# A state-space scan between an FFN and an attention on one Trainium2 core: fixed order on four engines, a quarter of the scaling as products with diagonals, and the last batch's softplus summed by TensorE

## The chip, the cores and the metric

The kernel runs on one core of one Trainium2 chip. The metric is the device time of one execution in microseconds (us). The engines are TensorE (PE, with its weight loads as PEld), VectorE (DVE), ScalarE (ACT), GpSimd (POOL) and SyncE (SP, which here only issues DMAs).

## The reference, cut to what matters

Four sublayers follow each other, each with a layer norm in front and a residual around it: a causal attention, a gated FFN with ternary weights, a selective state-space scan, and a second attention with a mixture of experts. All is float32. The change concerns the scan and what prepares it. B = 4 batches of T = 512 tokens with C = 512 channels, 16 states per channel:

```python
xz = einsum('btd,rd->btr', u, W_xproj)          # u = layernorm(x); 128 + 16 + 16 columns
delta = softplus(einsum('btr,dr->btd', xz[..., :128], W_dt) + b_dt)
dA = exp(delta[..., None] * -exp(A_log))        # [b, t, d, n]
Bu = delta[..., None] * B_mat[:, :, None, :] * u[..., None]
h_t = dA_t * h_(t-1) + Bu_t                     # along the 512 tokens
y_t = sum_n h_t * C_t[:, None, :]
x = x + y + u * D_param
```

## The kernel before, in words

The residual stream stays in SBUF as `xs[b]`, tokens on partitions: four tiles of 128 tokens by 512 channels per batch. The scan works on channels by tokens, since the scan instruction runs along the free dimension.

**FFN (L593 to L706).** One batch after another, eleven slices `f` of the hidden width. `gated` (L643) puts 16 matmuls into a pair of PSUM banks (the PSUM holds two such pairs and four single banks), then SiLU, product and casts follow on ACT and DVE; `down` (L663) multiplies by w2 one slice later. Between the slices, a generator `prepare` (L494) for the batch before is advanced by a number of steps that the list in L690 gives, and from slice 4 on also `inputs` (L610) for the next batch. Only PE's order is the program's; on the other engines a scheduler places the instructions.

**`prepare(b)`** normalizes the batch into `row_s` and adds u * D to x on POOL (L507, L508), transposes to `uT`, multiplies by W_xproj (`pd` of 128 rows, `pb` of 32 rows, L528), transposes the B columns to tokens (`pbt`, L539) into `bts`, and stores the C rows to DRAM (`c_rows`). Softplus is computed as max(z, 0) + ln(1 + e) with e = exp(-|z|), with the rounding of 1 + e put right: `e` from Abs and Exp on ACT (L551, L554), max(z, 0) in `delta` (L552), u = (e + 1) - 1 (L558), e - u (L559), added (L560), ln (L562), added (L567). delta goes to DRAM (`deltas`), delta * uT (`ux`, L570) is transposed and goes to DRAM as `dxs`. For the last batch `prepare` runs during the scan (L887), one step for every second scan step (L912).

**Scan (L805 to L954).** The eight PSUM banks are single: four for the sums of a batch, four for the rest. There are 128 steps (b, n, half): 4 batches, 16 states, and two halves of the channels. For each (b, n), `scale` (L823) runs eight instructions on ACT: four scalings of the token tiles of `dxT` by the B column (`bu`, L829) and four exponentials for dA (`da`, L835; two buffers). For each step, `turn` (L838) transposes 2 x 4 blocks into two banks; `scan` (L848) runs two scan instructions on DVE; `weigh` (L856) multiplies both by the C row (`cb`, a broadcast load from `c_rows`, L859) on POOL into `hc`; `add_up` (L867), two steps behind, transposes eight blocks on PE and sums them over n in the four banks, which are added to x at a batch's end (L882). `h` and `hc` have three buffers. `fetch` (L816) loads `delta_l` and `dxT` of a batch, 1 MB each; the first is asked for after the FFN (L884), the others at n = 3 of the batch before.

The order within the scan: PE's is written out (L889); DVE, ACT and POOL are placed by the scheduler, and SP's queue of DMAs too. From step 56 on the preparation's room is given to the next attention's weights (L918 to L949, 14 DMAs), and from step 78 on `enter` (L715) of the second attention's batch 0 is advanced at every third step: statistics, rows, squares, and transposes of its input.

Of the kernel before, what the change touches and what calls it, by code (L numbers as in the profile page):

```python
# [15 lines left out]
ALU = mybir.AluOpType  # L16
# [29 lines left out]
def block_kernel(ctx: ExitStack, tc: tile.TileContext, a: dict, out: bass.AP):  # L46
# [45 lines left out]
    deltas = tc.dram_tile([B, C, T], F32, name="deltas")  # L92
    dxs = tc.dram_tile([B * T, C], F32, name="dxs")


# [385 lines left out]
    dpar = sw.tile([P, C], F32, tag="dpar", name="dpar")  # L481

    def scan_constants(pool):

        nc.scalar.activation(am, am, AF.Exp)
        nc.vector.tensor_scalar(am, am, -1.0, None, ALU.mult)
        dp = half_pair("dp")
        for k in range(NK):
            diag = pool.tile([P, P], F32, tag="diag", name="diag")
            nc.vector.tensor_scalar(diag, ident, dcol[:, k : k + 1], None, ALU.mult)  # L490
            nc.tensor.matmul(dp[:, k * P : (k + 1) * P], ones, diag, start=True, stop=True)
        nc.scalar.copy(dpar, dp)

    def prepare(b, pool, spot, ahead):  # L494
# [29 lines left out]
        yield  # L524

        pb = spot("pb")
        for k in range(NK):
            nc.tensor.matmul(  # L528
                pb[: 2 * NS, :], wx[:, k, RANK:], uT[:, k, :], start=k == 0, stop=k == NK - 1
            )  # L530
            if k == 1:
                yield
        bcT = pool.tile([2 * NS, T], F32, tag="bcT", name="bcT")
        nc.scalar.copy(bcT, pb[: 2 * NS, :])
        nc.sync.dma_start(c_rows[b], bcT[NS:, :])
        yield
        pb = spot("pbt")
        for t in range(NT):
            nc.tensor.transpose(  # L539
                pb[:, t * NS : (t + 1) * NS], bcT[:NS, t * P : (t + 1) * P], ident[:NS, :NS]  # L540
            )
        nc.scalar.copy(bts[:, b, :], pb[:, : NT * NS])
        yield
# [43 lines left out]
        yield  # L587

    def half_pair(name):
        return pair(name)[:, 0, :]  # L590


    with tc.tile_pool(name="b_s", bufs=1) as bs, tc.tile_pool(name="b_1", bufs=1) as b1, tc.tile_pool(  # L593
# [16 lines left out]
        def inputs(b, mv=None):  # L610

            high = b2.tile([P, NK, T], F32R, tag="hTh", name="hTh")
            low = b2.tile([P, NK, T], F32R, tag="hTl", name="hTl")
            high_low[b] = high, low
# [56 lines left out]
        with tc.manual_schedule(engines={mybir.EngineType.PE}):  # L671
# [4 lines left out]
            for b in range(B):  # L676
# [7 lines left out]
                for f, rows in enumerate(FROWS):  # L684
                    pending.append((f, rows, gated(b, f, rows, hT)))
                    if b == 0 and f + 3 < NF:
                        quantize_down(f + 3)
                    if b == 0 and f == 6:
                        clear()
                    for _ in range((2, 3, 2, 2, 2, 3, 3, 3, 3, 4, 3)[f]):  # L690
                        next(between, None)
                    if f >= 4:
                        next(coming, None)
                    if b == 0 and f == 4:
                        scan_constants(b2)
                    if len(pending) > lag:
                        if ys is None:
                            ys = [bank(f"y{t}") for t in range(NT)]
                        down(b, *pending.pop(0), ys)
# [14 lines left out]

    def enter(b, pool):  # L715

# [16 lines left out]
        hT = far.tile([P, NK, T], F32, tag="hT", name="hTd")  # L733
        before = None
        for t in range(NT + 1):
            row = None
            if t < NT:
                row = pool.tile([P, C], F32, tag="row", name="row_d", bufs=2)
                nc.vector.scalar_tensor_tensor(
                    row, hs[b][:, t, :], rs[:, t : t + 1], ln1, ALU.mult, ALU.mult  # L740
                )
            if before is not None:
                transpose_into(hT, before, (t - 1) * P)
            before = row
            yield
# [59 lines left out]
    eight("s")  # L805
    with tc.tile_pool(name="c_f", bufs=2, reuse_waits="tile") as cf, tc.tile_pool(
        name="c_1", bufs=1
    ) as c1, tc.tile_pool(name="c_2", bufs=2) as c2:

        das = [c1.tile([P, NK, T], F32, tag=f"da{i}", name=f"da{i}") for i in range(2)]  # L810
        for da in das:
            nc.vector.memset(da[:, :, 0:1], 0.0)
        steps = [(b, n, half) for b in range(B) for n in range(NS) for half in range(2)]
        loaded, scaled, decays, turned, states, weighed, sums = {}, {}, {}, {}, {}, {}, {}

        def fetch(b):  # L816
            delta = cf.tile([P, NK, T], F32, tag="delta_l", name="delta_l")
            nc.sync.dma_start(delta, by_rows(deltas[b]))
            dxT = cf.tile([P, NT, C], F32, tag="dxT", name="dxT")
            nc.sync.dma_start(dxT, by_tokens(dxs, b))  # L820
            loaded[b] = delta, dxT

        def scale(b, n):  # L823

            delta, dxT = loaded[b]
            rows = []
            for t in range(NT):
                row = c2.tile([P, C], F32, tag=f"bu{t}", name=f"bu{t}")
# [8 lines left out]

        def turn(b, n, half):  # L838
            bu = [bank("bu") for _ in range(2)]
            for i in range(2):  # L840
                k = 2 * half + i
                for t in range(NT):
                    nc.tensor.transpose(  # L843
                        bu[i][:, t * P : (t + 1) * P], scaled[b, n][t][:, k * P : (k + 1) * P], ident
                    )
            turned[b, n, half] = bu

# [19 lines left out]
        def add_up(b, n, half):  # L867
# [3 lines left out]
            for i in range(2):  # L871
                k = 2 * half + i
                for t in range(NT):
# [5 lines left out]
                    )  # L879
            if n == NS - 1 and half == 1:  # L880
                for t in range(NT):
                    nc.vector.tensor_tensor(xs[b][:, t, :], xs[b][:, t, :], sums[b][t], ALU.add)  # L882

        fetch(0)  # L884
        last = ExitStack()
        cp = last.enter_context(tc.tile_pool(name="c_p", bufs=1, side="right", reuse_waits="tile"))
        between = prepare(B - 1, cp, bank, 4)  # L887
        come = enter(0, c1)
        with tc.manual_schedule(engines={mybir.EngineType.PE}):  # L889
            for _ in range(2):  # L890
                next(between)
            scale(0, 0)
            for _ in range(5):
                next(between)
            turn(*steps[0])
            for m, (b, n, half) in enumerate(steps):
                if half == 0:
                    if n + 1 < NS:
# [5 lines left out]
                if m + 1 < len(steps):  # L904
                    turn(*steps[m + 1])
                scan(b, n, half)
                weigh(b, n, half)
                if m >= 2:
                    add_up(*steps[m - 2])

                if m % 2 == 1:
                    next(between, None)  # L912
                if m == 56:
                    for _ in between:
# [34 lines left out]
                    ln1 = held("ln1", [P, C], a["ln1_w"].partition_broadcast(P))  # L949

                if m >= 76 and m % 3 == 0 and m < 76 + 3 * 13:
                    next(come)
            for step in steps[-2:]:
                add_up(*step)  # L954


# [538 lines left out]
```

## Time and profile before

| | us |
|---|---|
| Four runs: median (lowest, highest) | 1977.81 (1973.01, 1981.5) |
| Profiled execution: own time | 1977.9 |
| Profiled execution: span of the profile | 1976.2 |
| FFN's last matmul ends | 757.55 |
| First scan instruction starts | 768.98 |
| Step 58 starts (its first scan, the 117th) | 943.5 |
| Last scan instruction ends | 1120.1 |

All points in time are counted from the start of the span. A row of a table of busy times gives a stretch, its length, and the busy time of each engine with its instructions in brackets. A row of a timeline gives the start, the time until the last of the merged instructions ends, the engine, the line, the operation with output and inputs, and their number; in square brackets the idle time before it and who ended it. Instructions of one engine overlap a little, so prices are taken from start to start. In PE's rows a float32 matmul stands as two records and a transpose as one. Lines are of the kernel before unless the changed kernel is named.

### The profile page before, as it was taken

To read this page: it belongs to the slowest core of one execution; us is meant where nothing else is said; L and a number is where in the kernel's file an instruction comes from. 1 tells how busy PE (TensorE), PEld (TensorE's weight loads), DVE (VectorE), ACT (ScalarE), POOL (GpSimd) and SP (SyncE) were. 2 spreads that over 40 slices of the span, in tenths; PEclk is the share of its full clock that TensorE was granted. 3 is DMA by queue.
4 is the path that set the end of the run, shared out by engine and by line. 5 is a ranking of instruction groups with operands and counts; after the bars stand their busy time and mean duration, and the time that the engine had idled before them with its cause. 6 is when DMAs were issued, how large, how long until landed. Compare 5 with 4: busy or idle time off the path is not lost. (4 is left out here: it accounts for less than half of the span.)

```text
span 1976.2 us, 26953 instructions
## 1 busy us (share of the span) xinstructions
PE 1798.0 (91%) x10030; PEld 1084.9 (55%) x10030; DVE 1151.9 (58%) x1909; ACT 946.6 (48%) x1941; POOL 581.1 (29%) x390
## 2 busy tenths in 40 slices
PE   7999999989999897867887889999999999999997
PEld 3443343347666665656776655555565554545453
DVE  6456445675463737999999856664636543422223
ACT  3434433332243436978999646655646442111110
POOL 3221212110202205868998710001000000144431
PEclk9999999999999999989999979999979889999999
DMA  7003200110010104134311100010100106244446
GB/s 242 8 1 105 61 1 1 44 45 31 1 43 1 43 1 157 47 107 121 109 55 49 28 1 1 7 38 1 44 11 28 38 22 202 80 92 90 92 74 191
DMA packets 70885, 114.25 MB, mean 58 GB/s; under 512 B 7962, under 2 KB 26778, under 8 KB 70756
## 3 DMA queue, kind: packets, MB, share of 16 engines
q1 hardware_dynamic: 59796, 88.02, 13.7%
q0 software_dynamic: 8656, 20.32, 5.5%
q10 hardware_dynamic: 2304, 4.20, 0.6%
q8 instruction: 81, 1.33, 0.3%
q14 instruction: 48, 0.39, 0.1%
HBM read 81.18 MB, written 31.33 MB: 57 GB/s over the span
## 5 line engine op out<-in xcount | busy, mean ns | idle before, releaser
L862 POOL TENSOR_TENSOR hc<-h,cb 128x1024 f32<-128x1024 f32 x128 | 303.4, 2422 | 42.4 <-DVE h L851 26.3
L851 DVE TENSOR_TENSOR_SCAN h<-da,bu 128x512 f32<-128x512 f32 x256 | 290.0, 1197 | 14.4 <-ACT da L835 8.2
L843 PE MATMUL bu<-ident,bu 128*128 128x128 f32 x1024 | 163.8, 286 | 59.4 <-DVE h L851 36.0
L270 PE MATMUL pq<-wqkv,hT 128*128 128x512 f32 x384 | 181.8, 622 | 1.1 <-ACT hT L131 1.1
L843 PEld LDWEIGHTS bu<-ident,bu 128*128 128x128 f32 x1024 | 119.2, 144 | 94.3 <-ACT bu L829 55.1
L835 ACT ACTIVATE da<-delta_l,am 128x511 f32<-128x511 f32 x256 | 164.9, 723 | 3.6 <-DVE h L851 3.6
L829 ACT ACTIVATE bu<-dxT,bts 128x512 f32<-128x512 f32 x256 | 164.8, 723 | 0.5 <-PE bu L843 0.5
L875 PE MATMUL ys<-ident,hc 128*128 128x128 f32 x1024 | 140.8, 281 | 12.2 <-POOL hc L862 9.1
L1080 ACT ACTIVATE pr<-scd,nm 128x128 f32<-128x128 f32 (+3 forms) x256 | 133.0, 527 | 35.1 <-DVE nm L1077 31.1
L648 PE MATMUL pg<-hTh,w 128*128 128x512 f32 (+1 forms) x352 | 139.7, 397 | 2.9 <-DVE sil L654 2.1
L648 PE MATMUL pg<-hTl,w 128*128 128x512 f32 (+1 forms) x352 | 139.1, 395 | 0.2 <-DVE hTl L638 0.2
L1382 PE MATMUL pgr<-wgu,gTe 128*128 x304 | 137.1, 593 | 0.0
L875 PEld LDWEIGHTS ys<-ident,hc 128*128 128x128 f32 x1024 | 118.6, 145 | 20.9 <-POOL hc L862 16.1
L1069 PE MATMUL scd<-qkTd 32*128 32x512 f32 (+3 forms) x512 | 117.3, 541 | 12.2 <-ACT pr L1080 9.3
L270 PEld LDWEIGHTS pq<-wqkv,hT 128*128 128x128 f32 x384 | 72.3, 197 | 95.8 <-issue 87.1
L350 ACT ACTIVATE pt<-sc 128x1024 f32<-128x1024 f32 (+3 forms) x128 | 84.1, 698 | 83.8 <-PE sc L345 81.3
L1092 PEld LDWEIGHTS tpd<-ident,pr 128*128 128x128 f32 x640 | 74.7, 152 | 68.7 <-issue 35.8
L1092 PE MATMUL tpd<-ident,pr 128*128 128x128 f32 x640 | 109.0, 305 | 2.1 <-DVE ptd L1097 1.5
L101 POOL TENSOR_TENSOR ri_ln<-ri_ln,minus_half 128x4 f32<-128x4 f32 (+1 forms) x17 | 16.9, 994 | 308.0 <-DVE ri_ln L100 303.9
L1077 DVE TENSOR_REDUCE nm<-scd 128x2 f32<-128x256 f32 (+3 forms) x128 | 104.2, 814 | 0.0
L1072 DVE TENSOR_TENSOR scd<-scd,neg 128x256 f32<-128x256 f32 x128 | 54.9, 430 | 81.9 <-PE scd L1069 79.3
L351 POOL TENSOR_SCALAR_AFFINE_SELECT pt<-pt 128x512 f32<-128x512 f32 x64 | 43.4, 679 | 194.7 <-ACT pt L350 194.7
(258 smaller groups left out, 3164.6 us busy)
## 6 DMA issues: line engine op xcount, KB each, us to landing
cb<-c_rows SPq DMA_DIRECT2D x64, 256.0 KB, 3.2
q_w<-in_w2T SPq DMA_DIRECT2D x20, 256.0 KB, 2.9
deltas<-delta SPq DMA_DIRECT2D x16, 256.0 KB, 2.1
dxs<-st SPq DMA_DIRECT2D x16, 256.0 KB, 2.5
delta_l<-deltas SPq DMA_DIRECT2D x4, 1024.0 KB, 9.8
dxT<-dxs SPq DMA_DIRECT2D x4, 1024.0 KB, 6.9
acc<-h SPq DMA_DIRECT2D x16, 256.0 KB, 2.0
hrows<-h SPq DMA_DIRECT2D x4, 1024.0 KB, 4.3
```

Source lines behind the costliest of these rows:

```text
L270: nc.tensor.matmul(y, inputs_T[b][:, k, t * P : (t + 1) * P], wqkv[:, k, s * C : (s + 1) * C], start=k == 0, stop=k == NK - 1,)
L648: nc.tensor.matmul(pg[:rows, i, :], w[:, k, f * P : f * P + rows], part[:, k, :], start=k + m == 0, stop=k + m == NK,)
L829: nc.scalar.activation(row, dxT[:, t, :], AF.Copy, scale=bts[:, b, t * NS + n : t * NS + n + 1])
L835: nc.scalar.activation(da[:, k, 1:], delta[:, k, 1:], AF.Exp, scale=am[:, k, n : n + 1])
L843: nc.tensor.transpose(bu[i][:, t * P : (t + 1) * P], scaled[b, n][t][:, k * P : (k + 1) * P], ident)
L851: nc.vector.tensor_tensor_scan(h[:, i, :], decays[b, n][:, 2 * half + i, :], bu, 0.0, ALU.mult, ALU.add)
L862: nc.gpsimd.tensor_tensor(hc, states.pop((b, n, half)), weighed[b, n].unsqueeze(1).to_broadcast([P, 2, T]), ALU.mult)
L875: nc.tensor.matmul(sums[b][t][:, k * P : (k + 1) * P], hc[:, i, t * P : (t + 1) * P], ident, is_transpose=True, start=n == 0 and k == 0, s ...
L1069: nc.tensor.matmul(sc[:, i, :w], qkT[at, g, t * P : w], qkT[at, NG + g, :w], start=True, stop=True)
L1080: nc.scalar.activation(pr[:, i, :w], sc[:, i, :w], AF.Exp, bias=nm[:, i : i + 1], accum_out=sums[b, g][:, t, 2 * p + i : 2 * p + i + 1],)
L1092: nc.tensor.transpose(tp[:, j * P : (j + 1) * P], pr[:, i, j * P : (j + 1) * P], ident)
L1382: nc.tensor.matmul(pg, gT[:, k, :], wgu[:, bass.ds(e, 1), k, :].rearrange("p e o -> p (e o)"), start=k == 0, stop=k == NK - 1,)
```

## The change

- During the scan, the order of PE, DVE, ACT and POOL is that of the program. SP's queue is still placed by the scheduler.
- Token tile 0 is no longer scaled on ACT. `keep_inputs` makes, for each n, the 128x128 diagonal of the B column of tile 0 (one DVE instruction of 128x2048 per batch), stores all to DRAM (`diags`, 1 MB per batch), and `scale` loads one (64 KB) per (b, n). `turn` then makes the first block as a float32 product of `dxT` with the diagonal, where it had a transpose. `turn` is split in two, with `add_up` in between.
- B and C columns come from 16 matmuls per batch of 128 columns in four groups of 32 rows (`latents`), with one transpose instead of four; the C rows go out in four DMAs instead of one.
- The last batch has its own `prepare_last`, advanced at three of four steps. It evacuates a bank one advance after PE has filled it. It leaves POOL out: u * D is a product with diagonals on PE, added to x from PSUM; the four terms of softplus are summed in PSUM by matmuls with the identity (and its negative for `over`).
- `large` is a pool that first holds the FFN's inputs and then the scan's; `fetch(0)` is called after the first slice of the last FFN batch. The list of L690 differs for the last batch.
- The sums of a batch are added to x at step 2 of the next (`finish`). `enter` takes 14 advances, at every fourth step from step 62 on, and evacuates its transposes one advance later. The weights' room is taken at step 58.

```diff
+    def fetch(b):
+        delta = large.tile([P, NK, T], F32, tag="one", name="delta_l")
+        nc.sync.dma_start(delta, by_rows(deltas[b]))
+        dxT = large.tile([P, NT, C], F32, tag="two", name="dxT")
+        nc.sync.dma_start(dxT, by_tokens(dxs, b))
+    def latents(pb, uT):
+        for k in range(NK):
+            for t in range(NT):
+                nc.tensor.matmul(
+                    pb[t * 2 * NS : (t + 1) * 2 * NS, :P], wx[:, k, RANK:], uT[:, k, t * P : (t + 1) * P],
+                    start=k == 0, stop=k == NK - 1,
+                )
+    def keep_inputs(b, pb, room):
...
+        diag = room.rearrange("p k t -> p (k t)").rearrange("p (n q) -> p n q", n=NS)
+        nc.vector.tensor_tensor(
+            diag, ident.unsqueeze(1).to_broadcast([P, NS, P]),
+            bts[:, b, :NS].unsqueeze(2).to_broadcast([P, NS, P]), ALU.mult,
+        )
+        nc.sync.dma_start(diags[b], diag)
...
-        for t in range(NT):
-            nc.tensor.transpose(
-                pb[:, t * NS : (t + 1) * NS], bcT[:NS, t * P : (t + 1) * P], ident[:NS, :NS]
-            )
-        nc.scalar.copy(bts[:, b, :], pb[:, : NT * NS])
+        nc.tensor.transpose(pb[:, :P], bcT, ident)
+        e = pool.tile([P, NK, T], F32, tag="e", name="diag_s")
+        keep_inputs(b, pb, e)
...
+    def prepare_last(b, pool):
...
+        terms = ((ident, relu), (ident, e), (minus, over), (ident, ln))
+        scaled = tp = None
+        for k in range(NK + 2):
+            if k >= 2:
+                st = pool.tile([P, NT, P], F32, tag="st", name="st")
+                nc.scalar.copy(st.rearrange("p t q -> p (t q)"), tp)
+                nc.sync.dma_start(by_tokens(dxs, b)[:, :, (k - 2) * P : (k - 1) * P], st)
+            if 1 <= k <= NK:
+                delta = pool.tile([P, T], F32, tag="delta", name="delta", bufs=2)
+                nc.scalar.copy(delta, pd)
+                nc.sync.dma_start(deltas[b, (k - 1) * P : k * P, :], delta)
+                scaled = pool.tile([P, T], F32, tag="ux", name="ux", bufs=2)
+                nc.vector.tensor_tensor(scaled, pd, uT[:, k - 1, :], ALU.mult)
+            if k < NK:
+                pd = bank("pdl")
+                for i, (w, term) in enumerate(terms):
+                    nc.tensor.matmul(pd, w, term[:, k, :], start=i == 0, stop=i == 3)
+                    if i % 2 == 0:
+                        yield
...
-                    for _ in range((2, 3, 2, 2, 2, 3, 3, 3, 3, 4, 3)[f]):
+                    pace = (3, 3, 3, 3, 3, 3, 3, 3, 3, 2, 0) if b == B - 1 else (2, 3, 2, 2, 2, 3, 3, 3, 3, 3, 3)
+                    for _ in range(pace[f]):
                         next(between, None)
+                    if b == B - 1 and f == 0:
+                        fetch(0)
...
         def scale(b, n):
             delta, dxT = loaded[b]
-            for t in range(NT):
+            diag = c1.tile([P, P], F32, tag="diag", name="diag_l", bufs=3)
+            nc.sync.dma_start(diag, diags[b][:, n, :])
+            rows = [diag]
+            for t in range(1, NT):
...
+        def turn(b, n, half, i):
+            bu = bank("bu")
+            k = 2 * half + i
+            nc.tensor.matmul(
+                bu[:, :P], loaded[b][1][:, 0, k * P : (k + 1) * P], scaled[b, n][0],
+                start=True, stop=True,
+            )
+            for t in range(1, NT):
+                nc.tensor.transpose(
+                    bu[:, t * P : (t + 1) * P], scaled[b, n][t][:, k * P : (k + 1) * P], ident
+                )
...
-        with tc.manual_schedule(engines={mybir.EngineType.PE}):
+        engines = {getattr(mybir.EngineType, e) for e in ("PE", "DVE", "Activation", "Pool")}
+        with tc.manual_schedule(engines=engines):
...
             for m, (b, n, half) in enumerate(steps):
+                if m % each == 2 and b > 0:
+                    finish(b - 1)
+                if m % 4 != 3:
+                    next(between, None)
+                if m >= 62 and m % 4 == 2 and m < 62 + 4 * 14:
+                    next(come)
...
                 if m + 1 < len(steps):
-                    turn(*steps[m + 1])
+                    turn(*steps[m + 1], 0)
                 scan(b, n, half)
                 weigh(b, n, half)
                 if m >= 2:
                     add_up(*steps[m - 2])
-                if m % 2 == 1:
-                    next(between, None)
-                if m == 56:
+                if m + 1 < len(steps):
+                    turn(*steps[m + 1], 1)
+                if m == 58:
```

In the first part of `prepare_last`, each advance gives PE four transposes of a row tile, one of the four matmuls of `pd`, the latents, one of the four matmuls of `pz` (512 columns each), or four 128x128 products for u * D; DVE gets statistics, `minus` and four diagonals `dd` of 128x128, rows, `relu` (max(z, 0) from PSUM) and `over` (the (e + 1) - 1 of before).

## The prediction

> **What bounds the kernel now.** I began with the page's engine shares. They name TensorE:
>
> ```profile
> PE 1798.0 (91%) x10030; PEld 1084.9 (55%) x10030; DVE 1151.9 (58%) x1909; ACT 946.6 (48%) x1941; POOL 581.1 (29%) x390
> ```
>
> This is an average over stages. The change lies in the scan, from the first scan instruction at 769.0 us to the end of the last at 1120.1 us, so I split that stage at step 58 of 128, where the preparation of the last batch has ended. Step 58 starts at 943.5: the first 58 steps took 174.5 us, the last 70 took 176.6. The table of busy times over two stretches close to these parts (columns: stretch, length, then busy us of PE, PEld, DVE, ACT, POOL, granted clock, DMA):
>
> ```profile
> 769.00:942.00 173.00, 133.34 (x952) 109.76 (x950) 165.00 (x156) 157.43 (x252) 139.94 (x62) 0.95 0.29 93
> 942.00:1121.00 179.00, 148.76 (x1142) 126.45 (x1142) 167.87 (x155) 171.62 (x285) 169.16 (x76) 0.99 0.20 63
> ```
>
> VectorE is full in the first part, ScalarE in the second, and PE is not the bound in either. The prices come from the timeline where each engine runs without a gap, one answer per engine:
>
> ```profile
> 934.61 28.96 DVE L851 TENSOR_TENSOR_SCAN h<-da,bu 128x512 f32<-128x512 f32 x26
> ...
> 932.91 35.12 POOL L862 TENSOR_TENSOR hc<-h,cb 128x1024 f32<-128x1024 f32 x15
> ...
> 954.33 2.55 ACT L835 ACTIVATE da<-delta_l,am 128x511 f32<-128x511 f32 x4
> 956.78 2.56 ACT L829 ACTIVATE bu<-dxT,bts 128x512 f32<-128x512 f32 x4
> 959.23 2.56 ACT L835 ACTIVATE da<-delta_l,am 128x511 f32<-128x511 f32 x4
> ```
>
> A scan costs 1.114 us from start to start, two per step: 2.23. POOL's product costs 2.34 per step. ScalarE's eight instructions per two steps take 959.23 - 954.33 = 4.90, or 2.45 per step. **ScalarE is the slowest of the three**, and 70 x 2.45 = 171.5 plus the next attention's copies and squares (about 5) is the second part's 176.6.
>
> **The scan, part by part.** ScalarE loses one scaling in eight: 7/8 x 2.45 = 2.15 per step. From there POOL, then VectorE, are slowest, and what ScalarE still does (58 x 2.15 = 124.5, plus some 18 us of copies, exponentials and table loads in the first part) is covered by both.
>
> TensorE takes over the scaling: two transposes per step become float32 products 128x128 by 128. No product of this kind stands in the scan. Its price follows from matmuls among the transposes:
>
> ```profile
> 780.58 1.88 PE L519 MATMUL pd<-uT,wx 128*128 128x512 f32 x4
> 782.29 1.04 PE L843 MATMUL bu<-ident,bu 128*128 128x128 f32 x8
> 783.17 1.04 PE L875 MATMUL ys<-ident,hc 128*128 128x128 f32 x8
> 784.04 1.09 PE L843 MATMUL bu<-ident,bu 128*128 128x128 f32 x8
> ```
>
> Eight transposes take 0.87: 0.109 each. Four records of 512 columns take 1.71; two are one matmul, so 0.86, and going over to transposes costs nothing visible. For 128 columns the record falls to the transposes' own 0.109 (32 records of 76 columns at L1332 take 3.5), so a product is 0.22. A step becomes 14 x 0.109 + 2 x 0.22 = 1.96, under 2.23: hidden. Its cover is gone where more matmuls come in.
>
> *Start.* Before, the inputs are asked for only at 756.6, when the FFN ends:
>
> ```profile
> 762.85 1.28 ACT L835 ACT_TABLE_LOAD   x1 [6.70 <-DMA delta_l<-deltas]
> ```
>
> and the first scan comes at 768.98. After, both loads are queued behind the first gated pair of the last FFN batch. ScalarE then does three scalings, the table load and four exponentials (7 x 0.61 + 1.28 = 5.6) after its last FFN cast, which ends at 753.9: ready at 759.5. VectorE finishes x[3] at 758.9 and has two statistics in front of the scan (1.4): 760.3. The diagonal's load is queued on SP behind the last dxs stores. If its room frees with the last FFN matmul (757.5) it lands by the row of cb, 3.2 later, and PE needs 0.55: 761.3. Saved: 8; bounds 9 and 4 (a load that waits like cb's slowest, 8.6). I take **-8.0**.
>
> *Steps 0 to 57, VectorE.* 116 scans x 1.114 = 129.2. Beside them: two statistics 1.4, root and five 128x128 diagonals 1.6 (L490: 0.28 each), four rows 2.5, the 128x2048 diagonal product 2.3 (L1314: 2.28), four maxima from PSUM 2.6, four `over` 1.7, the sums of batch 0 2.4, four additions of the D product 2.4, four `ux` 2.4: 19.3. Gone are the subtraction and the two additions of the softplus, and POOL's eight instructions for x*D. What remains is the price of the port:
>
> ```profile
> 837.22 0.76 DVE L558 TENSOR_SCALAR u<-e 128x512 f32<-128x512 f32 x1
> 838.02 2.74 DVE L559 TENSOR_TENSOR u<-e,u 128x512 f32<-128x512 f32 x1
> 840.79 0.69 DVE L560 TENSOR_TENSOR delta<-delta,u 128x512 f32<-128x512 f32 x1
> ```
>
> The same subtraction takes 0.69 when POOL has nothing to do, so 2.05 of the 2.74 are a wait while POOL multiplies; its neighbours lose nothing much. Operations that read PSUM never show it. After the change 15 operations of the kinds that waited (scalings and two-tensor forms on SBUF alone) stand in this part, in six groups. A group waits between 0 and 2.05; I take 1.2, the middle, since in this trace the first of a group often gets in ahead: 7.2. VectorE: 155.7.
>
> **A rule of the skill speaks against this**: "SBUF — State Buffer" in the Trainium skill, section "SBUF: two separate sides", says the port pair is an exclusive lock for the whole instruction, so each such operation may lose up to one whole product of POOL. The row agrees in kind (2.05 of 2.34) but shows one wait in three operations. By the rule at its worst the sum would be about rival C's.
>
> *PE in this part.* Each `next` of the preparation gives PE work: 16 matmuls of 0.86 for the softplus alone, between steps 40 and 53. There PE needs 14 x 1.96 + 16 x 0.86 + 3 x 0.44 = 42.5, VectorE 14 x 2.23 + 4 x 0.6 = 33.6: PE is late by 8.9. In steps 12 to 18 PE has four 0.86 and the latents (about 2): 19.2 against 15.6, 3.6 more. With four PSUM banks for `bu` and preparation neither can run ahead, so both count: 12.5; bounds 4 and 15. Sum 168.2 against 174.5: **-6.3** (bounds -15 and +6).
>
> *Steps 58 to 127.* VectorE: 140 x 1.114 = 156.0, two sums 4.8, the next attention's statistics, rows and products 7.7: 168.5 before waits. POOL: 70 x 2.341 + two powers of 1.02 + 4.5 in which VectorE's ten port operations hold it = 170.4. Both near each other: 172.5. SP has 14 weight loads in one run ahead of the diagonal of n = 31 and its cb, 0.47 each to issue (6.6) and about 5 to land, with some 9 us of steps to hide in; I charge 2 (bounds 0 and 8). 174.5 against 176.6: **-2.1** (bounds -7 and +8).
>
> *FFN, three batches.* The latents before: 3.62 in PE; after, 32 records of 128 columns in four column groups, between 0.058 (32 records of `avd` in 1.87) and 0.109: 1.9 to 3.5. Three transposes less, 0.33, and the 0.59 that `pz` waited for `bts`. Against it: the diagonal product of 2.28 on VectorE, idle half of the time here, then 1 MB from `e`'s room (hrows: 4.3 to land; delta_l: 9.8), on which ScalarE's first Abs waits; behind it stand the two PSUM pairs that the gated matmuls need too. Loss 0 to 4.5 a batch; I take 1.5, near the 4.3 row. Together **-1.0** (bounds -7 and +6).
>
> **Sum.** -8.0 - 6.3 - 2.1 - 1.0 = -17.4. The profiled execution took 1977.9 (span 1976.2 and 1.7 around it), and the median of the four runs is 1977.81, so no shift is needed: **1960.5**.
>
> **Rivals.**
> - *A, only the start is won.* ScalarE's relief is of no use because VectorE is bound all along. For: 165 of 173 us busy. Against: idle time before scans in the second part is mostly ScalarE's `da` (6.9 us). The stage keeps 351: 1977.9 - 8 - 1 = 1969.
> - *B, the fixed order hides all waits.* First part 148.5 + 5, second 170.4: 324 instead of 351, so 1977.9 - 27 - 8 - 3 = 1940. For: POOL and VectorE did run gapless for 35 us at 932.9. Against: the PE sum for steps 40 to 53.
> - *C, the port; slower.* POOL's products slip in between any two of VectorE's 25 port operations, and a queue in fixed order cannot put a scan there. All 25 whole: 30.8 instead of 7.2 in the first part, 168.5 + 20.5 = 189 instead of 172.5 in the second, +40: 2000. The gain is gone from about 14 whole waits on. Against: one in three above.
> - *D, no change.* FFN and the weight loads at their upper bounds (+7, +6): 1973.5.
>
> **How the numbers follow.** Forecast 0.40 (1954 to 1966), A 0.20, B 0.16, D 0.12, C 0.12. A change under 0.3% (5.9 us) can't be told from none. A lies mostly below 1971.9: faster 0.40 + 0.16 + 0.18 = 0.74, same 0.14, slower 0.12. The range 1943 to 1982 leaves out the far ends of B and most of C.
>
> **What would show it.** The distance from the FFN's last matmul (end 757.55) to the first scan shrinks from 11.4 to about 3.5; three scalings per n on ScalarE (L978 of the changed kernel); ScalarE with gaps; POOL's products back to back at 2.34 after step 62; PE gapless and VectorE idle in steps 40 to 53; PE's wait for diagonal 31 near step 61. Wrong if a product with a diagonal costs 0.4 or more (PE then bounds every step), or if `pz` waits longer than 5 us in an FFN batch.

## The result and the profile after

The changed kernel takes 1976.05 us (median of 44 runs; the kernel before 1976.73 of 70): the ratio measured is 1.0005 with an interval of 0.9993 to 1.0017 (the two medians alone would give 0.9997). No difference can be measured. The forecast was 1960.5, with a chance of 0.74 for faster. The profiled execution has a span of 1978.7 us (before 1976.2).

Since the granted clock of the long part behind the scan differs from one execution to the next (last section), I read the stage itself, in four stretches: *start* (from the FFN's last update of x to the first scan), *part 1* (to step 58), *part 2* (to the end of the last scan) and *tail* (to the addition to x). All come from the times in the trace of one execution per kernel. The rows below the second are those of the experiments.

| kernel | start | part 1 | part 2 | tail | sum |
|---|---|---|---|---|---|
| before | 12.76 | 174.52 | 176.58 | 4.35 | 368.2 |
| after | 4.26 | 177.87 | 186.36 | 5.30 | 373.8 |
| e1 loads spread | 4.26 | 176.11 | 176.95 | 5.72 | 363.0 |
| e2 no diagonals | 4.25 | 170.98 | 187.65 | 4.03 | 366.9 |
| e3 before + early loads | 13.07 | 174.42 | 176.62 | 4.46 | 368.6 |
| e4 port operations moved | 4.33 | 167.04 | 187.92 | 5.87 | 365.2 |
| e6 = e1 + e4 | 4.25 | 167.75 | 177.10 | 5.27 | 354.4 |
| e7 = e1 + e2 | 4.26 | 171.42 | 185.18 | 4.98 | 365.8 |
| e9 = e6 + rows on ScalarE | 4.32 | 167.03 | 176.87 | 5.30 | 353.5 |
| e10 = e3 + first turn ahead | 11.33 | 183.56 | 176.75 | 4.61 | 376.3 |
| e11 = e10 + pace and rooms | 5.44 | 186.64 | 176.22 | 4.05 | 372.4 |
| e12 = e1, placed order from step 60 | 4.26 | 182.15 | 173.68 | 5.85 | 365.9 |
| e13 = e12, no diagonals | 4.25 | 176.60 | 175.26 | 4.32 | 360.4 |
| e15 = e1, softplus summed by VectorE | 4.26 | 186.94 | 177.06 | 5.86 | 374.1 |
| e16 = e6, two terms left out | 4.25 | 159.73 | 179.64 | 5.85 | 349.5 |

The start came 8.50 us sooner, as forecast, and part 1 lost 3.35 of it, part 2 9.78 and the tail 0.95. First the table of busy times of the kernel after, over stretches like those shown of before (columns as there):

```profile
770.00:942.00 172.00, 157.50 (x1171) 138.44 (x1172) 156.88 (x141) 135.78 (x219) 134.70 (x57) 0.94 0.28 86
942.00:1121.00 179.00, 152.24 (x1212) 136.00 (x1211) 168.37 (x161) 149.34 (x245) 160.23 (x70) 0.97 0.30 90
```

In the second stretch ScalarE fell from 171.62 to 149.34: the diagonals did relieve it. No engine is busy for the whole of a stretch any more, and yet nothing became shorter. Where part 2 stands still is seen in the timelines of VectorE, PE and SP's queue of the kernel after (SPq rows are DMA issues):

```profile
955.09 1.22 DVE L1004 TENSOR_TENSOR_SCAN h<-da,bu 128x512 f32<-128x512 f32 x1 [7.83 <-PE bu L996]
```
```profile
943.98 0.49 PE L996 MATMUL bu<-ident,bu 128*128 128x128 f32 x3
953.54 0.77 PE L991 MATMUL bu<-diag_l,dxT 128*128 128x128 f32 x2 [9.07 <-DMA diag_l<-diags]
```
```profile
938.49 0.33 SPq L1078 DMA_DIRECT2D ln<-in_ln_w  x1
...
945.14 0.50 SPq L1090 DMA_DIRECT2D ln<-in_ln_w  x1
945.75 1.37 SPq L974 DMA_DIRECT2D diag_l<-diags  x2
```

The 14 weight loads hold SP's queue from 938.49 to 945.75; the diagonal that PE wants at 944.5 is asked for only then and lands 7.7 us later. Every scan behind it is late by as much. For the rest of part 2 VectorE is nearly without a gap (0.79, 0.61 and 0.17 us of idle time), and it has more to do there than before. Before, the scheduler had placed the next attention's statistics and normalized rows ahead of step 58, 9.4 us of VectorE between 886 and 926; after, all of them stand behind it. So the parts of before and after do not compare one by one, only their sum does (351.1 before, 364.2 after); the forecast had put this work into part 2. Two of these rows before, and one after:

```profile
893.57 1.81 DVE L100 TENSOR_SCALAR ri_ln<-mv_d 128x4 f32<-128x4 f32 x1
922.53 3.25 DVE L725 TENSOR_SCALAR h<-x,mv_d,ri_ln 128x512 f32<-128x512 f32 x2
```
```profile
987.79 2.03 DVE L101 TENSOR_SCALAR ri_ln<-mv_d 128x4 f32<-128x4 f32 x1
```

In part 1 the loss is made of two kinds of rows, here of VectorE's timeline after:

```profile
765.86 3.00 DVE L634 TENSOR_SCALAR dd<-ident,dcol 128x128 f32<-128x128 f32 x4
773.24 3.07 DVE L639 TENSOR_SCALAR row_s<-x,mv,ri_ln 128x512 f32<-128x512 f32 x2
778.48 3.02 DVE L639 TENSOR_SCALAR row_s<-x,mv,ri_ln 128x512 f32<-128x512 f32 x2
823.48 3.81 DVE L516 TENSOR_TENSOR diag_s<-ident,bts 128x2048 f32<-128x2048 f32 x1 [1.10 <-ACT bts L511]
851.70 3.46 DVE L688 TENSOR_SCALAR over<-e 128x512 f32<-128x512 f32 x2
859.54 3.15 DVE L688 TENSOR_SCALAR over<-e 128x512 f32<-128x512 f32 x2
893.03 0.69 DVE L718 TENSOR_TENSOR ux<-pdl,uT 128x512 f32<-128x512 f32 x1 [3.32 <-ACT delta L715]
904.38 0.69 DVE L718 TENSOR_TENSOR ux<-pdl,uT 128x512 f32<-128x512 f32 x1 [1.12 <-ACT delta L715]
```

The first six contain waits that stand as busy time: without one, four `dd` would take 0.7, two rows 1.2, the diagonals' product 2.28 and two `over` 0.86, so the six lose 2.3, 1.9, 1.8, 1.5, 2.6 and 2.3, together about 12.4. The two `ux` start 0.03 to 0.04 us after ScalarE's copy of the same bank ends. That copy waits for PE in turn: in the first for the last of the four terms, in the second for the transposes behind the terms, whose copy stands in front of it on ScalarE, while the terms are ready (modelled end 902.80) before VectorE's scan ends (903.27). ScalarE's timeline after:

```profile
903.28 0.60 ACT L711 COPY st<-tpd 128x512 f32<-128x512 f32 x1 [1.70 <-PE tpd L728]
903.76 0.59 ACT L715 COPY delta<-pdl 128x512 f32<-128x512 f32 x1
```

So PE's queue is at the root of these waits, and the order of ScalarE's two copies passes them on; no run has another order of the copies.

### The profile page after: what moved, and what is told of

Its sections match the earlier page's. It is cut to its first block, busy times and chain, and to the rows that moved or that the text cites. A ratio compares the mean times of both kernels' runs of the same rounds, so it can differ in the third digit from the quotient of the medians.

```text
span 1978.7 us, 27743 instructions
## 1 busy us (share of the span) xinstructions
PE 1819.0 (92%) x10434; PEld 1125.8 (57%) x10434; DVE 1156.7 (58%) x1910; ACT 910.2 (46%) x1884; POOL 571.1 (29%) x382
## 5 line engine op out<-in xcount | busy, mean ns | idle before, releaser
L978 ACT ACTIVATE bu<-dxT,bts 128x512 f32<-128x512 f32 x192 | 124.3, 712 | 31.9 <-PE bu L996 31.9
L991 PE MATMUL bu<-diag_l,dxT 128*128 128x128 f32 x512 | 106.9, 292 | 31.2 <-DVE h L1004 19.8
L996 PE MATMUL bu<-ident,bu 128*128 128x128 f32 x768 | 133.2, 282 | 2.2 <-ACT bu L978 1.9
L991 PEld LDWEIGHTS bu<-diag_l,dxT 128*128 128x128 f32 x512 | 81.8, 199 | 48.1 <-DVE h L1004 27.0
L996 PEld LDWEIGHTS bu<-ident,bu 128*128 128x128 f32 x768 | 97.3, 147 | 4.6 <-ACT bu L978 4.5
```

The lines of the kernel that those rows point to most:

```text
L978: nc.scalar.activation(row, dxT[:, t, :], AF.Copy, scale=bts[:, b, t * NS + n : t * NS + n + 1])
L991: nc.tensor.matmul(bu[:, :P], loaded[b][1][:, 0, k * P : (k + 1) * P], scaled[b, n][0], start=True, stop=True,)
L996: nc.tensor.transpose(bu[:, t * P : (t + 1) * P], scaled[b, n][t][:, k * P : (k + 1) * P], ident)
```

## The experiments

**e1: loads spread.** The 14 loads are put on a list and issued one per step from step 58 on.

```diff
-                    nc.sync.dma_start(ln2, a["ln2_w"].partition_broadcast(P))
+                    later(ln2, a["ln2_w"].partition_broadcast(P))
...
+                if loads:
+                    nc.sync.dma_start(*loads.pop(0))
```

> The changed kernel, with the 14 weight loads of step 58 issued one per step over steps 58 to 71. Theory 1 (SP's queue: the diagonal of n = 31 waits for 14 issues): the idle times of 7.83 and 0.95 us before scans near 950 us vanish, step 58 to the last scan goes from 186.3 to about 177.5, and the time from 1976 to about 1967.5 (ratio to the kernel before 0.9955). Rival (the transfers themselves crowd the DMA engines, wherever they are issued): the wait is spread over more steps and the sum stays within 3 us of the changed kernel, 1973 to 1976.

Measured: 1974.36, ratio 0.998 (0.9958 to 1.0001). Part 2 went from 186.36 to 176.95, and both idle times are gone: theory 1 in the stage. In the whole time its ratio of 0.9955 lies 0.0003 outside the interval, and 1974.36 lies in the rival's span; but the rival's reason, a wait spread over more steps, is not there, with 1.6 us of idle time left on VectorE in all of part 2. SP asks for the same diagonal at 939.66 here, behind two weight loads only:

```profile
938.79 0.44 SPq L1113 DMA_DIRECT2D wr<-in_router_w  x1
939.66 0.33 SPq L974 DMA_DIRECT2D diag_l<-diags  x1
```

**e2: no diagonals**, from the kernel after; **e7: the same with the loads spread.**

```diff
-            diag = c1.tile([P, P], F32, tag="diag", name="diag_l", bufs=3)
-            nc.sync.dma_start(diag, diags[b][:, n, :])
-            rows = [diag]
-            for t in range(1, NT):
+            rows = []
+            for t in range(NT):
```

> The changed kernel without diagonals: four scalings on ScalarE, four transposes on TensorE, nothing stored or loaded for diagonals. Theory 1 (ScalarE's relief is worth nothing, since VectorE stands right behind it): step 58 to the last scan 177 to 180 (ScalarE 70 x 2.45 + 5 = 176.5, VectorE 168.5 + 7.5 of port waits; no late diagonal), the first part 172 to 176 (3.8 us less on VectorE for the diagonals' product, and TensorE relieved of 58 x 0.22 = 12.8), the time about 1964 to 1968. Rival (the relief pays, and the late diagonal only hides it): ScalarE is the bound again with its own waits, the second part stays at 184 to 188, and the time at 1972 to 1978.

> The changed kernel with the weight loads spread and without diagonals (both edits of the first experiments together), which takes from the run without diagonals the wait for cb behind the same 14 loads. Theory 1 (ScalarE's relief is worth nothing; the block of loads is what cost): first part 171 as without diagonals, second part 177 to 179 (ScalarE 70 x 2.45 + 5 = 176.5), the time 1963 to 1967. Rival (the diagonals pay in the second part): second part 183 to 188, the time 1970 to 1976.

Measured: e2 1972.41, ratio 0.9977 (0.9957 to 0.9998); e7 1961.75, ratio 0.9935 (0.9904 to 0.9965). Part 1 fell by 6.9 in e2, below theory 1's 172 to 176, and by 4.7 between e1 and e7. Part 2 did not fall: in e2 the load of `cb` waits behind the same block (POOL idle 7.12), and in e7, without the block, it is still 185.18. My theory that ScalarE's relief is worth nothing fell here, in a fixed order. ScalarE's timeline of e7 shows what it loses there:

```profile
982.09 0.63 ACT L867 ACTIVATE sq_d<-h 128x512 f32<-128x512 f32 x1 [4.02 <-POOL hc L1001]
994.14 0.63 ACT L867 ACTIVATE sq_d<-h 128x512 f32<-128x512 f32 x1 [1.51 <-DVE h L863]
1016.51 0.63 ACT L867 ACTIVATE sq_d<-h 128x512 f32<-128x512 f32 x1 [1.42 <-DVE h L863]
1054.10 2.56 ACT L968 ACTIVATE bu<-dxT,bts 128x512 f32<-128x512 f32 x4 [2.08 <-PE bu L982]
```

ScalarE is nearly full (173.35 of 185.18); the squares of the next attention wait for VectorE's rows and for what holds those, the scalings stand behind them in order, and the four waits make 9.0 us. With diagonals ScalarE has the slack for that. VectorE is as full (179.43 busy, against 175.38 in e1): two of the four rows that the squares wait for took 3.27 instead of some 0.9, behind POOL's products, so ScalarE and VectorE hold each other, and the 8.2 of difference to e1 can't be put down to ScalarE alone. VectorE's timeline of e7:

```profile
990.84 3.27 DVE L863 TENSOR_SCALAR h<-x,mv_d,ri_ln 128x512 f32<-128x512 f32 x1
```

The whole time of e7 is lower than its stage explains: in its profile the FFN, which no longer makes the diagonals, ended 3.7 earlier, and the rest, without any edit, was 7.1 shorter than in the kernel after. I hold only the stage lengths against each other.

**e3: the early loads alone, in the kernel before.**

```diff
+                    if b == B - 1 and f == 0:
+                        fetch(0)
...
-        fetch(0)
         last = ExitStack()
```

> The kernel before, with nothing of the change but the shared room and the first loads of delta and dxT during the FFN. Theory 1: the first scan comes 7 to 9 us earlier and nothing else changes: about 1968.5 (ratio 0.996). Rival (the start is given back inside the scan in any case, since ScalarE is the bound of the second part and the work is only waited for later): 1974 to 1977.

Measured: 1977.92, ratio 0.9998 (0.9977 to 1.0019). Near the rival's number, but not for its reason: the first scan itself did not come sooner (13.07 after the update). What stood in front was something else, which e10 and e11 look for.

**e10: the first turn ahead of the preparation, too.**

```diff
-            for _ in range(2):
-                next(between)
             scale(0, 0)
-            for _ in range(5):
-                next(between)
             turn(*steps[0])
...
-                if m % 2 == 1:
+                if m % 2 == 1 or m < 14:
                     next(between, None)
```

> The kernel before with the early loads (as in the run that had nothing but them, where the first scan came 13.07 us after the FFN's last update began, against 12.76 before), and with the first turn ahead of the seven advances of the preparation in TensorE's order; the seven are made at steps 0 to 13. Theory 1 (the early load alone is worth nothing because TensorE's order put rows, statistics and transposes of the preparation ahead of the first turn; both together are the gain): the first scan 4 to 6 us after the update, the first part 174 to 178, the time 1968 to 1974. Rival (VectorE's placed order or ScalarE holds the first scan too): first scan still 10 or more us after the update, the time 1975 to 1979.

Measured: 1976.67, ratio 0.9996 (0.9978 to 1.0014); first scan after 11.33: the rival. Part 1 rose by 9.1 over e3's. ScalarE waited for the DMA that empties a room of the FFN's preparation, and VectorE had four rows in front (ScalarE's and VectorE's timelines of e10):

```profile
762.22 2.56 ACT L834 ACTIVATE bu<-dxT,bts 128x512 f32<-128x512 f32 x4 [2.93 <-DMA dxs<-st]
```
```profile
764.09 3.84 DVE L121 TENSOR_SCALAR row_s<-x,mv,ri_ln 128x512 f32<-128x512 f32 x4 [1.20 <-POOL ri_ln L101]
```

**e11: pace and rooms, too.**

```diff
-                    for _ in range((2, 3, 2, 2, 2, 3, 3, 3, 3, 4, 3)[f]):
+                    pace = (3, 3, 3, 3, 3, 3, 3, 3, 3, 3, 0) if b == B - 1 else (2, 3, 2, 2, 2, 3, 3, 3, 3, 4, 3)
...
-        name="c_1", bufs=1
+        name="c_1", bufs=1, reuse_waits="tile"
```

> The kernel before with the early loads and the first turn ahead of the preparation (where the first scan came 11.33 us after the FFN's last update began, ScalarE waiting to 762.2 for the last dxs stores to leave the rooms that it writes), and in addition the last FFN batch's preparation advanced one slice earlier and the scan's small rooms released tile by tile. The placed order now has the first scans ahead of the rows on VectorE, and exponentials between ScalarE's last FFN instructions. Theory 1 (the start is won by four edits together: load, order, pace, rooms): first scan 4 to 7 us after the update. Rival (the 3.8 us of rows and the table loads still stand in front): 9 us or more. What part 1 makes of it in a placed order is open: 174 to 185.

Measured: 1984.92, ratio 1.0035 (1.0012 to 1.0059): slower. The first scan came 5.44 after the update, theory 1. But the update itself came at 765.07 instead of 756.51 in e10, and part 1 rose to 186.64 (e10: 183.56). The lateness begins in the first slices of the last FFN batch: the second SiLU there starts at 688.4 (e10: 682.0). With the preparation one slice earlier, PE waits for its rows, and from 680 to 690 the granted clock is 0.66, where it is 1.00 in e10 (PE's timeline and the table of busy times of e11):

```profile
681.39 1.08 PE L130 MATMUL tp<-ident,row_s 128*128 128x128 f32 x4 [3.41 <-DVE row_s L121]
```
```profile
680.00:690.00 10.00, 7.72 (x27) 6.18 (x28) 5.27 (x5) 1.91 (x4) 8.95 (x7) 0.66 0.01 2
```

The placed order also put exponentials around the last SiLU, with two more loads of ScalarE's tables, but they add little: the SiLU before them is 8.1 us later than in e10, the last one 8.2. ScalarE's timeline of e11:

```profile
757.20 1.28 ACT L841 ACT_TABLE_LOAD   x1
758.50 0.72 ACT L841 ACTIVATE da<-delta_l,am 128x511 f32<-128x511 f32 x1
759.24 1.28 ACT L663 ACT_TABLE_LOAD   x1
760.53 0.68 ACT L663 ACTIVATE sil<-pg,sc_w 85x512 f32<-85x512 f32 x1
```

So neither the loads alone (e3) nor loads and order (e10) win the start; with pace and rooms it is won, but the late update gave stores and loads 8.6 us more time in e11, so which of the two does it is not shown. In these two kernels part 1 takes back more: in e10 as idle time of VectorE (17.0 against 8.1 in e3), in e11 mostly as its busy time (174.4 against 166.3).

**e4: port operations moved.** `minus` and `dd` are made in the FFN, rows and `over` (two instructions each) go to ScalarE, and the diagonals' product reads the B columns from PSUM. **e6: with the loads spread.**

```diff
-            nc.vector.tensor_scalar(over[:, k, :], e[:, k, :], 1.0, -1.0, ALU.add, ALU.add)
+            nc.scalar.activation(over[:, k, :], e[:, k, :], AF.Identity, bias=1.0)
+            nc.scalar.activation(over[:, k, :], over[:, k, :], AF.Identity, bias=kept["one"])
...
-            bts[:, b, :NS].unsqueeze(2).to_broadcast([P, NS, P]), ALU.mult,
+            pb[:, :NS].unsqueeze(2).to_broadcast([P, NS, P]), ALU.mult,
```

> The changed kernel, with VectorE's SBUF-only operations of the first part taken away: minus and dd are made in the FFN, the four rows and the four over (two instructions each) go to ScalarE, and the diagonals' product reads the B columns from PSUM. Theory 1 (port waits of 12.4 us and the operations' own 8 us lie on VectorE's path): the first part falls from 177.9 to 160 to 168, the time to 1958 to 1968. Rival (TensorE bounds the first part: 157.5 busy of 172, and its peaks come in the last preparation): the first part stays at 174 to 178, the time at 1973 to 1977.

> The changed kernel with the weight loads spread and with the first part's port operations off VectorE (the two edits of the first experiments together). Theory 1 (the two costs are separate and add): first part 167, second part 177, the time about 1957 (ratio to the kernel before 0.990). Rival (what is saved in the first part only lets a later wait come sooner): the sum of the parts stays above 350 and the time at 1968 to 1976.

Measured: e4 1974.48, ratio 0.9982 (0.9966 to 0.9999); e6 1957.39, ratio **0.9903 (0.9879 to 0.9926)**, with e9 the lowest among the versions that sum all four terms. Part 1 fell by 10.83 in e4, inside theory 1's span; e4's whole time missed and lies in the rival's span, since in part 2 the same diagonal was now waited for 9.22 and 1.53: part 1 came sooner, and the loads did not. With both edits the gains in the stage add as forecast (10.8 and 8.6 make 19.4). Against the kernel before, the stage alone would give ratios of 0.9974 for e1, 0.9985 for e4 and 0.9930 for e6: the first two lie in the measured intervals, and e6 is a little faster than its stage explains. The product with its B columns in PSUM, in e4 (3.81 after):

```profile
816.80 2.29 DVE L516 TENSOR_TENSOR diag_s<-ident,pbt 128x2048 f32<-128x2048 f32 x1 [1.10 <-ACT bts L511]
```

**e9: the next attention's normalized rows on ScalarE, too.**

```diff
-            nc.vector.tensor_scalar(
-                hs[b][:, t, :], xs[b][:, t, :], mv[:, t, 0:1], rs[:, t : t + 1], ALU.subtract, ALU.mult
-            )
+            nc.scalar.activation(
+                hs[b][:, t, :], xs[b][:, t, :], AF.Identity, scale=rs[:, t : t + 1], bias=shift[:, t : t + 1]
+            )
```

> As the kernel with spread loads and without the first part's port operations; in the second part also the four normalized rows of the next attention go from VectorE to ScalarE (4 x 0.69 and their port waits). Theory 1 (VectorE bounds the second part): second part 172 to 174 against 177, the time about 1953. Rival (POOL, 70 x 2.34 and what holds it, stands right behind VectorE): second part 175 to 177, the time 1956 to 1958.

Measured: 1960.72, ratio 0.9913 (0.9891 to 0.9936); part 2 176.87. Neither theory: the rival's part 2, but POOL is busy for 166.32 of it. VectorE's busy time fell by 3.6 and its idle time rose by as much: now ScalarE waits in its order (4.29 for a small operand of VectorE) and VectorE for ScalarE's `da` and squares (0.89, 0.94, 2.88).

**e12: from step 60 on only TensorE's order written out; e13: the same without diagonals.** Both have the loads spread.

```diff
+                if m == 60:
+                    order.close()
+                    order.enter_context(tc.manual_schedule(engines={mybir.EngineType.PE}))
```

> The changed kernel with the weight loads spread; from step 60 on only TensorE's order is written out, and VectorE, ScalarE and POOL are placed by the scheduler as in the kernel before. Theory 1 (with diagonals ScalarE has slack, so the order from step 60 on matters little): second part 174 to 180. Rival (the fixed order costs waits behind small operations): second part 168 to 173.

> The same without diagonals: four scalings on ScalarE, weight loads spread, a placed order from step 60 on. Theory 2, formed after the run without diagonals but with a fixed order gave 185.2 in the second part (ScalarE is full there, and in a fixed order it loses about 9 us waiting for VectorE's rows ahead of its squares; in a placed order it had other work in front): second part 176 to 179. Rival (the diagonals themselves pay those 8 us): second part 183 to 187.

Measured: e12 1973.58, ratio 0.9983 (0.9961 to 1.0005); e13 1964.18, ratio 0.994 (0.9916 to 0.9964). The scheduler drew the next attention's statistics and first rows into part 1, so here too only the sums of both parts compare:

| | fixed order | placed from step 60 |
|---|---|---|
| with diagonals | 353.1 (e1) | 355.8 (e12) |
| without | 356.6 (e7) | 351.9 (e13) |

e12's 173.68 lies between the spans of its two theories, e13's 175.26 just under theory 2's. The diagonals win 3.5 where the order is fixed and lose 4.0 where it is placed, and the fixed order costs 4.7 without them: in these single profiles they buy back about what the fixed order costs.

**e15: the softplus summed by VectorE** again, on e1.

```diff
-                    nc.tensor.matmul(pd, w, term[:, k, :], start=i == 0, stop=i == 3)
+                nc.vector.tensor_tensor(over[:, k, :], e[:, k, :], over[:, k, :], ALU.subtract)
+                nc.vector.tensor_tensor(relu[:, k, :], relu[:, k, :], over[:, k, :], ALU.add)
...
-                nc.scalar.copy(delta, pd)
+                nc.vector.tensor_tensor(delta, relu[:, k - 1, :], ln[:, k - 1, :], ALU.add)
```

> The changed kernel with the weight loads spread, and the last batch's softplus summed by VectorE again (subtraction, two additions, ux from SBUF; no identity products). Theory 1 (12 more operations of 0.69 on the port, each behind POOL's product: 8.3 + about 18; TensorE's late terms, 9 us, go): first part 188 to 195 against 176.1, the time 1984 to 1990. Rival (TensorE's peak costs as much as VectorE's additions): first part 172 to 179, the time 1969 to 1976.

Measured: 1978.67, ratio 1.0019 (0.9991 to 1.0048); part 1 186.94, 1 us under theory 1's span and far from the rival's. Summing by TensorE is worth 10.8 us. VectorE's timeline of e15 shows one whole wait in each group (ux 2.74 and 2.76 against 0.69) and 0 to 0.25 in a single operation behind a scan (e7's rows of 3.27 were single, too, so this is no rule):

```profile
893.83 0.66 DVE L714 TENSOR_TENSOR delta<-relu,ln 128x512 f32<-128x512 f32 x1
894.53 2.74 DVE L717 TENSOR_TENSOR ux<-delta,uT 128x512 f32<-128x512 f32 x1
...
902.25 0.91 DVE L721 TENSOR_TENSOR relu<-relu,over 128x512 f32<-128x512 f32 x1
...
908.51 2.76 DVE L717 TENSOR_TENSOR ux<-delta,uT 128x512 f32<-128x512 f32 x1
```

**e16: two of the four terms left out**, on e6 (8 of 16 matmuls).

```diff
-        terms = ((ident, relu), (ident, e), (minus, over), (ident, ln))
+        terms = ((ident, relu), (ident, ln))
```

> As the kernel with spread loads and without the first part's port operations (first part 167.75: TensorE 154.0 busy, VectorE 146.2), with two of the four terms of the last batch's softplus left out (e and over, the correction of the rounding of 1 + e is not applied): 8 matmuls of 512 columns fewer on TensorE, 6.9 us. Theory 1 (TensorE's terms are what VectorE waits for once the port is clear): first part 160 to 163, the waits of 3.3 and 1.1 us before ux shrink to under 1. Rival (other engines and the scans themselves set the pace there): first part 166 to 168.

Measured: 1954.45, ratio 0.9864 (0.9827 to 0.9902); part 1 159.73, 8.0 less than e6 for 6.9 of matmuls: theory 1. The first wait before `ux` is gone from VectorE's timeline and the others, 1.1 each, are 0.25 to 0.3; of the 8.0, part 2 gave back 2.5.

```profile
891.01 0.69 DVE L725 TENSOR_TENSOR ux<-pdl,uT 128x512 f32<-128x512 f32 x1 [0.25 <-ACT delta L722]
```

## Why the prediction was wrong

Forecast was a gain of 17.4 us. In the profile the stage became 5.6 longer: the start came as forecast, and two terms of the scan were sized too low, a wait for POOL in part 1 and the late diagonal with VectorE's own work in part 2.

*Start, -8.0: right.* 8.50, and from the end of the FFN's last matmul (756.7) to the first scan it is 2.9 (forecast about 3.5). What I did not see is that the early loads alone are worth nothing (e3), nor with the first turn put ahead (e10).

*FFN, -1.0: not refuted.* The last update starts at 755.36 against 756.21. Four profiles with the FFN of the kernel after (after, e1, e12, e15) lie between 755.4 and 758.1, so 1 us can't be resolved.

*Steps 0 to 57, -6.3: wrong, +3.35.* The step that failed is "A group waits between 0 and 2.05; I take 1.2, the middle". The six groups waited 12.4 where I had 7.2: 2.07 each, the upper end. The trace of before had it already: of its four groups of `u`, `u` and `delta`, three lost a whole product, the one shown above and these two, which is 1.5 a group and not 1.2.

```profile
827.46 2.75 DVE L559 TENSOR_TENSOR u<-e,u 128x512 f32<-128x512 f32 x1
846.92 2.75 DVE L560 TENSOR_TENSOR delta<-delta,u 128x512 f32<-128x512 f32 x1
```

"One wait in three operations" is one wait in each group, in a placed order too; whether the fixed order adds to it no run tells apart. e4 took these waits away, and most of the operations with them: VectorE's busy time in part 1 fell by 16.5 (162.7 to 146.2), and part 1 by 10.8, since idle time took its place (15.2 to 20.8). TensorE's excess was sized about right: 12.5 forecast, 14.8 of idle time on VectorE measured. In steps 40 to 53 PE was idle for 0.5 of 43.4 us (42.5 forecast) and VectorE for 8.8 (8.9 forecast); in e16, on top of e6, fewer terms shorten part 1 by what they cost. Of the 9.7 missed, 5.2 are the port, 2.3 idle time, and 2.2 I can't attribute.

*The rule of the skill.* "SBUF — State Buffer" in the Trainium skill, section "SBUF: two separate sides", says that a VectorE operation with two SBUF inputs or in a two-port mode and a GpSimd operation shut each other out for whole instructions. The runs agree in kind: a wait of 1.5 to 2.6 per group, where a product of POOL takes 2.34, and none where an input comes from PSUM (3.81 became 2.29 in e4, although POOL multiplied until 818.46). They do not bear out the worst case that the prediction took from it, a whole wait for every operation: six in 15 operations.

*Steps 58 to 127, -2.1: wrong, +9.78.* The step that failed is "I charge 2 (bounds 0 and 8)". It cost 7.83 + 0.95 in the profile, and 9.4 by e1. The 6.6 of issues was right; the landing took 7.7 and not 5, and the steps that could hide it were worth 6 and not 9. The rest, 176.95 in e1 against the 172.5 that I took, is VectorE: 175.4 busy where I had 168.5 before waits. The term behind it is "the next attention's statistics, rows and products 7.7": they took 14.8 in e1, with waits in them (the row at 987.79 above took 2.03, the same operation at 765.67 took 0.14). Before, VectorE was busy for 166.4 of part 2, since the scheduler had 9.4 of this work in part 1. So ScalarE's relief found VectorE with more to do, and 176.58 became 176.95. That is what rival A names; against it I held "idle time before scans is mostly ScalarE's": who ends the idle time does not say how near the next engine is.

*Rivals.* The time is near D's by chance: of its two upper bounds only the weight loads' was met, and passed. A's mechanism, VectorE as the bound, holds in part 2 once the loads are spread; that the relief is worth nothing does not follow, as e7 shows. C named a real cost at well over twice its size (25 whole waits would be 51.3; about 19 us were measured, 12.4 in part 1 and, as VectorE's busy time above the 168.5, 6.9 in part 2). B's first part of 153.5 is not reached even in e16.

*Open.* The stage is 5.6 longer in the profile, the medians 0.7 apart with an interval of about 2.4 either way. The FFN and the rest, 0.85 and 2.2 shorter there, leave 2.5 of it in the span; whether they are so by the change or by the clock isn't settled. Nor is why e7 and e13 have shorter times than their stages explain.

## What to carry to other kernels

Before relieving the engine that is full, add up the next one with its waits: here ScalarE's 176.58 became VectorE's 176.95. Say also where the work around a stage will stand: a scheduler may have put it into a gap that a written order leaves empty. A transfer that a step needs is as late as everything in front of it in its queue; count the issues from the queue's rows, and spread loads that nobody waits for. Where operations of one engine wait for long instructions of another, count the waits by group in the whole trace and not in the one row at hand: here it was one whole wait a group, three times in four before and six times in six after.

## What the hardware showed beyond that

- The part behind the scan, which no edit touched, ran at a granted clock that differs between executions, and took 840.8 us (e10, granted clock 0.95, PE busy 794) to 858.0 (e15, 0.93, PE busy 812). PE is busy for 95% of it, and a spread of 17 us there hides effects of a few us in the whole time; the lengths of the stages repeat within 1 us (part 2 at 176.95, 177.06 and 177.10 in e1, e15 and e6).
- A 64 KB load landed in 7.7 us behind 14 weight loads, against 3.3 and 2.7 for the diagonals asked for at 931.05 and 958.83.
- Going from exponential to SiLU and back cost ScalarE 1.28 us for each table, without further idle time (e11).
